# V of the later sequences by seven half-depth products, with its bias added by a transfer and its tokens turned by VectorE

## The chip, the cores and the metric

The kernel runs on one core of one Trainium2 chip. A core has five engines with instruction queues of their own: TensorE (PE; its weight loads are shown apart as PEld), VectorE (DVE), ScalarE (ACT), GpSimd (POOL) and SyncE (SP), which here only issues transfers. Sixteen DMA engines move data between the chip's memory (HBM) and the on-chip buffers. Matmul results go to PSUM, of which this kernel uses eight banks of 128 x 512 float32 in turn. The metric is the device time in microseconds, the median of several executions. The profile comes from one further execution; its span reaches from the first to the last instruction.

## The reference

Four sequences of 2048 tokens with 512 columns pass through one transformer block: layer norm, attention with 16 heads of 32 columns, and beside it two experts out of eight, chosen by the first token of each sequence. All is float32.

```python
xn = layernorm(x)                                  # x: 4 x 2048 x 512
q, k, v = split(xn @ qkv_w.T + qkv_b)              # 16 heads of 32
att = softmax(q @ k.T / sqrt(32)) @ v
o1 = att @ proj_w.T + proj_b
e = top_2(xn[:, 0] @ Wr + br)                      # two experts for each sequence
o2 = mean over e of (gelu(xn @ W1[e] + b1[e]) @ W2[e] + b2[e])
out = x + o1 + o2
```

## The kernel before

**Units.** The attention is cut into 1024 units. A unit is one group of four heads, one chunk of 512 queries and one tile of 128 keys; 16 units make a chunk, 64 units a group (four chunks), 256 units a sequence (four groups). One loop over `U` (L898) writes out every engine's instructions in order (the schedule is by hand), from 22 lead-in steps below zero to 1023. In a unit TensorE lays the negative maxima into four PSUM banks by a bf16 product (`shift`, L773), adds the scores (`score`, L781), and computes the plain scores of a unit 22 steps later (`score_max`, L763), whose maxima VectorE takes (L925). ScalarE makes the exponentials `p` (L918). In even units TensorE weighs V with the two latest `p` tiles (`weigh`, L793). POOL adds up the `p` tiles of a chunk (`add_weights`, L804 to L820); the last tile of a chunk is added by an accumulating transfer instead (L818). `add_keys` (L822) then sums over the keys on TensorE, four or five units into the next chunk. There are four `p` buffers.

**Dense items.** Odd units (and lead-in steps) are slots for one dense item each, after the attention's own work: projections `qk` and `v`, the experts' `w1` and `w2`, and the output projection `proj`. `Plan` (L38) fixes the slots of `qk` and `v`, and fills the rest from two queues of parts in order of their due times; some slots stay empty, spread evenly over slots at the sixth unit of a chunk (`rests`). Every item issues its matmuls in fours side by side (`product`, L499): four weight loads of 32 columns each, each with a moving operand of 512 columns. An fp32 matmul of the program is two matmul instructions in the profile.

**Seven products.** `qk` and `w1` are already computed with seven instead of eight half-depth products of 2 x 2 blocks. The combined blocks of tokens (`tx`, `token_blocks`) and weights (`ws`, `weight_blocks`) are made by POOL and stored to HBM; a product loads its two blocks (`load_xt`, `load_wt`) and `combine` (L535) adds the result into the outputs. `GAPS` (L31) lists which products share a slot. V is not done so: `project_v` (L526) takes all 512 rows of depth in one product for 128 tokens, adds the bias on VectorE (L532) and stores 256 KB to `v_dram`, from where each group loads its 128 columns (`v`, four buffers).

**The next sequence's tokens.** While a sequence is in its second and third group, the next one is normalised: statistics (`stats`), one square root for all (`root`, L450), `normal` on ScalarE, and `turn` (L469): four transposes of 128 x 128 on TensorE into a bank, a copy by VectorE (L474) into a staging tile, and at a chunk's end a store of 1 MB to `xn_dram`. ScalarE must load another function table for the square root and for Gelu, and again for the exponential (`back_to_exp`, L690).

**Planned loads.** Each load is issued by SyncE, in order, up to eight units ahead of its use or when its buffer comes free (`loads`, L225). What is to be stored goes through `later`, one to four units behind its work. The rows that collect the output get their biases in HBM by an accumulating transfer on POOL's queue (`add_bias`, L697).

Of the kernel before, what the change touches and what calls it, by code (L numbers as in the profile page):

```python
# [30 lines left out]
GAPS = [[(1, 0)], [(1, 1)]] + [[(i, 0), (i, 1)] for i in (6, 7)]  # L31
GAPS += [[(5, h), (3, h)] for h in (0, 1)] + [[(i, 0), (i, 1)] for i in (4, 2)]
COMBINED = (0, 1, 1, 2)
STORED = 6
# [3 lines left out]
class Plan:  # L38
# [5 lines left out]

    def __init__(self, B, DC, NCH, NT, TPC):
        self.per_group = NCH * NT
# [12 lines left out]
        for G in range(1, B * DC):  # L59
            b, g = divmod(G, DC)  # L60
            first = (G - 1) * self.per_group
            for n, products in enumerate(GAPS):
                at = (11, 12, 13, 14, 15, 16, 17, 19) if g else (5, 6, 7, 8, 9, 11, 12, 13)
                fixed[first + 2 * at[n] + 1] = ("qk", b, g, products)
            if g == 0:
                at = [n for n in range(14, 32) if n % 8 != 2]
                for t in range(NT):
                    fixed[first + 2 * at[t] + 1] = ("v", b, t)
        v_stored = {}
        for s, item in fixed.items():  # L70
            if item[0] == "v":
                v_stored[item[1], item[2] // TPC] = s + 3
        for b in range(B):
            for g in range(DC):
                for c in range(NCH):
                    self.first_load["v", (b, g, c)] = v_stored[b, c]
        for b in range(1, B):
# [8 lines left out]
            for n in range(NT):  # L86
                self.extra.setdefault(q1 + 2 * (16 + n) + 1, []).append(("stats", b, n))
                c, i = divmod(n, TPC)
                at = q2 + 2 * (1 + 18 * (c // 2) + 5 * (c % 2) + i) + 1
                self.extra.setdefault(at, []).append(("normal", b, n))  # L90
                self.extra.setdefault(at + 2, []).append(("turn", b, n))
            self.extra.setdefault(q2 + 1, []).append(("root", b, 0))
            for p in range(NCH // 2):
# [8 lines left out]
        for p, at in enumerate((slots[8], slots[16])):  # L102
            for n in range(4):
                self.extra.setdefault(at + n, []).append(("tx", 0, (p, n)))
            for i in STEPS:
                self.first_load["xt", (0, p, i)] = at + 5
        for k, at in enumerate((slots[2], slots[7])):
            for n in range(4):
                self.extra.setdefault(at + n // 2, []).append(("ws", 0, (k, n)))
            for i in STEPS:  # L110
                self.first_load["wt", ("w1", 0, k, i)] = at + 4
# [26 lines left out]
        free = [s for s in slots if s > 0 and s not in fixed]  # L138
        rests = [s for s in free if s % NT == 5]
        share = spare / len(rests)  # L140
        current, before, owed = [], None, 0
        for s in slots:
# [7 lines left out]
            )  # L150
            before = None
            if s in rests:
                owed += share
# [12 lines left out]
        for s in range(NT, self.units, NT):  # L166
            ends = s + NT == self.units
            self.keys_at[s // NT - 1] = 5 if s + 5 not in self.items and not ends else 4
        assert not fixed and not proj and not ffn and not current, (proj, ffn, current)

        rows_at = {}
        for s in slots:
            for it in self.items.get(s, []):
                if it[0] == "w2":
                    rows_at[it[1], it[3]] = s + 3
                assert it[0] != "proj" or s - 2 * WARN >= rows_at[it[1], it[2]], (s, it)
                for tag, key in self.needs(it):
# [7 lines left out]
        for s in range(slots[0], self.units):  # L185
            for kind, b, n in self.extra.get(s, []):
                if kind == "ws":

                    last = n[1] == 3
                    self.uses.append((s + (2 if b == 0 else 4) * last, "xl", ("w1raw", b, n[0])))  # L190
                elif kind == "tx" and b:
                    for c in (2 * n[0], 2 * n[0] + 1):
                        self.uses.append((s + 4 * (n[1] == 3), "xq", ("stage", b, c)))
                elif kind in ("stats", "normal"):
                    self.uses.append((s, "xl", (kind, b, n // TPC)))
                elif kind == "turn":
                    self.uses.append((s, "xq", ("stage", b, n // TPC)))
        self.uses.append((self.units, "wb", ("proj",)))
# [9 lines left out]
    def needs(item):  # L208
# [5 lines left out]
        if kind == "v":  # L214
            return [("wb", ("v",))] + ([("xq", (b, item[2] // TPC))] if b else [])
        if kind == "w1":
# [8 lines left out]
    def loads(self, bufs, start):  # L225
# [3 lines left out]
        for s, tag, key in self.uses:  # L229
# [9 lines left out]
            for t in tiles:  # L239
                if t[0] == key:  # L240
                    t[1] = s + 2 if tag in ("row", "prow") or tag == "xq" and key[0] == "stage" else s
        return {at: sorted(v, key=lambda e: e[0]) for at, v in out.items()}


@with_exitstack
def block_kernel(
# [45 lines left out]
    for b in range(B):  # L292
# [3 lines left out]
        tc.dram_tile([3, GH * TPC, TPC, HD], BF16, name=f"parts_dram_{n}") for n in range(2)  # L296
    ]
    wqk_dram = [tc.dram_tile([P, DC, D], F32, name=f"wqk_dram_{n}") for n in range(2)]
    for b in range(B):
        for c in range(NCH):  # L300
            xn_dram[b, c] = tc.dram_tile([P, DC, CH], F32, name=f"xn_dram_{b}_{c}")
            v_dram[b, c] = tc.dram_tile([P, TPC, D], F32, name=f"v_dram_{b}_{c}")
# [7 lines left out]
    BUFS = {"xq": 2, "xt": 4, "xl": 1, "wt": 4, "v": 4, "wb": 2, "row": 4, "prow": 2}  # L310
    held = {}
    experts = {}
# [9 lines left out]


    def load_xt(t, b, p, i):

        if i in (1, 2, 3):
            src, h = xn_dram[b, 2 * p + (i == 3)], int(i != 1)
        else:
# [3 lines left out]
    def load_wt(t, kind, b, n, i):  # L332


        r, h = {1: (0, 0), 2: (0, 1), 4: (1, 1), 6: (0, 0), 3: (0, 1), 7: (1, 0), 5: (1, 1)}[i]
        if kind == "qk":
            if i in (1, 2, 4):
# [15 lines left out]
    def load(tag, key):  # L353
# [4 lines left out]
        held[tag, key] = t  # L358
        if tag == "xq" and key[0] == "stage":
            return t  # L360
        if tag == "xq":
            nc.sync.dma_start(t, xn_dram[key])
        elif tag == "xt":
# [105 lines left out]
    def turn(dst, t, i, name):  # L469
# [4 lines left out]
        nc.vector.tensor_copy(dst[:, :, ts(i, P)], pt.rearrange("p (d t) -> p d t", d=DC))  # L474


    mv, sd, nb = stat_tiles("first")
# [57 lines left out]
    def combine(i, x, c, b1, b2, on_dve):  # L535

        add = nc.vector.tensor_tensor
        biased = nc.vector.scalar_tensor_tensor
        if i == 1 and on_dve:
# [7 lines left out]
        elif i == 5:  # L547
            biased(c[1, 1], x, b2, c[1, 0], ALU.add, ALU.add)
            add(c[0, 1], x, c[0, 1], ALU.add)
        else:  # L550
            at, b_ = {3: ((0, 1), b1), 4: ((1, 0), b2), 2: ((0, 0), b1)}[i]
            biased(c[at], x, b_, c[at], ALU.add, ALU.add)

# [25 lines left out]

    stage = {}  # L580

    def blocks(kind, b, n, U):


        if kind == "tx":
            p, n = n
# [20 lines left out]
    def dense(item, U, on_dve, between):  # L607
# [20 lines left out]
        elif kind == "v":  # L628
            n = item[2]
            project_v(b, n, tiles[1] if b else stage[0, n // TPC], tiles[0], U)  # L630
        elif kind == "w1":
# [83 lines left out]
    def first_turn(c):  # L715
# [5 lines left out]
        for i in range(TPC):  # L721
            turn(xn, x_first[c][:, i, :], i, f"0_{c}_{i}")
        nc.sync.dma_start(xn_dram[0, c], xn)

# [79 lines left out]
    def add_weights(u):  # L804
# [9 lines left out]
        elif kt == 1:  # L814
            psums[b, g, qc] = pair.tile([P, GH, CH], F32, tag="psum", name=f"psum_{b}_{g}_{qc}")
            nc.gpsimd.tensor_tensor(psums[b, g, qc], pT[u - 1], pT[u], ALU.add)  # L816
        elif kt == NT - 1:
            nc.gpsimd.dma_start(psums[b, g, qc], pT[u], accum_op=ALU.add)  # L818
# [69 lines left out]

    row_ready = {}
    loads = plan.loads(BUFS, -LEAD - 1)  # L890
# [7 lines left out]
    for U in range(-LEAD, plan.units):  # L898
# [43 lines left out]

        two = any(it[0] in ("qk", "w1") and len(it[-1]) == 2 for it in plan.items.get(U, []))
        if not two:
# [5 lines left out]
        if second:  # L950
            add_weights(U)
        for t in row_ready.pop(U, []):
            nc.gpsimd.tensor_tensor(t, t, bias[0], ALU.add)
# [5 lines left out]
        for u in (U - 2, U - 3):  # L959
            late = u + 3 < plan.units and u + 3 not in plan.items  # L960
            if u % 2 == 0 and u >= plan.units - NT and late == (u == U - 3):
                add_last(u)
        if before is not None and kt == keys:
            add_keys(before, bank("keys_%d_%d_%d" % before), [psums[before]], False)
        for step, sb, n in plan.extra.get(U, []):
            if step == "stats":
                if n == 0:
                    norms[sb] = stat_tiles(sb)
                stats(norms[sb][0], n, held["xl", ("stats", sb, n // TPC)][:, n % TPC, :])
            elif step in ("ws", "tx"):  # L970
                blocks(step, sb, n, U)
# [5 lines left out]
            else:  # L977
                c, i = divmod(n, TPC)
                xs = stage[sb, c] = held["xq", ("stage", sb, c)]
                turn(xs, held["xl", ("normal", sb, c)][:, i, :], i, f"{sb}_{n}")  # L980
                if i == TPC - 1:
                    later(U + 1, lambda sb=sb, c=c, xs=xs: nc.sync.dma_start(xn_dram[sb, c], xs))
        for item in plan.items.get(U, []):
            dense(item, U, curve is not None, invert if two else lambda: None)

# [111 lines left out]
```

## Time and profile before

| | us |
|---|---|
| median of three runs | 4973.19 (4972.93 to 4974.06) |
| the profiled execution | 4967.9 |
| its span | 4966.1 |
| mean granted TensorE clock, share of full | 0.999 |
| vector additions of psum on POOL, L820 | 3724.0 busy, 819 of 4.547 |
| accumulating transfers psum<-p, landing | 63, median 8.6 |
| DMA queue of SP, share of 16 engines' span | 31.7% |

The profile's busy time of a group is the union of its instructions' times, so side-by-side matmuls count once. In a row of a group the number behind the bar is busy time in microseconds and the mean of one instruction in ns; then the idle time of the engine ahead of the group, and what ended it. "vps" are V's results in PSUM, "xt" both the banks of turned tokens (L473) and the loaded token blocks, "xq" 1 MB buffers of tokens.

### The profile page before, as it was taken

To read this page: it belongs to the slowest core of one execution; us is meant where nothing else is said; L and a number is where in the kernel's file an instruction comes from. 1 tells how busy PE (TensorE), PEld (TensorE's weight loads), DVE (VectorE), ACT (ScalarE), POOL (GpSimd) and SP (SyncE) were. 2 spreads that over 40 slices of the span, in tenths; PEclk is the share of its full clock that TensorE was granted. 3 is DMA by queue.
4 is the path that set the end of the run, shared out by engine and by line. 5 is a ranking of instruction groups with operands and counts; after the bars stand their busy time and mean duration, and the time that the engine had idled before them with its cause. 6 is when DMAs were issued, how large, how long until landed. Compare 5 with 4: busy or idle time off the path is not lost.

```text
span 4966.1 us, 108027 instructions
## 1 busy us (share of the span) xinstructions
PE 4913.9 (99%) x44740; PEld 1712.0 (34%) x44740; DVE 3714.2 (75%) x5899; ACT 2491.9 (50%) x4570; POOL 4403.5 (89%) x1469
## 2 busy tenths in 40 slices
PE   8999999999999999999999999999999999999999
PEld 2333333333333333333333333333333333333332
DVE  5777787777777787777777778877777777777772
ACT  1445456464444545454455445555544445555553
POOL 2799999999898998999988998999988988989983
PEclk9999999999999999999999999999999999999999
DMA  6334337433333434634234244564423343323323
GB/s 225 113 106 120 112 99 196 150 121 110 82 107 104 131 109 139 187 122 137 88 94 132 73 128 128 171 167 131 145 70 98 106 129 107 95 81 112 87 81 101
DMA packets 327772, 594.93 MB, mean 120 GB/s; under 512 B 42220, under 2 KB 162540, under 8 KB 310384
## 3 DMA queue, kind: packets, MB, share of 16 engines
q1 hardware_dynamic: 311872, 509.37, 31.7%
q0 software_dynamic: 15408, 78.65, 8.2%
q8 instruction: 352, 5.77, 0.5%
q14 instruction: 140, 1.15, 0.1%
HBM read 380.81 MB, written 153.62 MB: 108 GB/s over the span
## 4 chain that ended last, share of the span: by engine, by line
PE 83%; ACT 6%; POOL 5%; issue 3%; DMA 2%; DVE 1%; SPq 0%; POOLq 0%; ACTq 0%
PE acc L793 17%; PE s L781 15%; PE m L763 15%; PE qkps L503 6%; PE ops L503 6%; PE hps L503 6%; PE s L773 6%; PE vps L503 5%; POOL psum L820 4%; PE prps L503 4%; ACT p L918 3%; DMA psum<-p 2%; PE keys L826 1%; ACT L692 1%; ACT h L922 1%
## 5 line engine op out<-in xcount | busy, mean ns | idle before, releaser
L820 POOL TENSOR_TENSOR psum<-psum,p 128x2048 f32<-128x2048 f32 x819 | 3724.0, 4547 | 158.3 <-ACT p L918 117.4
L918 ACT ACTIVATE p<-s 128x512 f32<-128x512 f32 x4096 | 2116.9, 602 | 2225.3 <-PE m L763 2062.8
L925 DVE TENSOR_REDUCE mx<-m 128x1 f32<-128x512 f32 x4096 | 2543.1, 683 | 569.2 <-PE m L763 567.4
L781 PE MATMUL s<-qT,kT 32*128 32x512 f32 x8192 | 1919.0, 588 | 0.0
L763 PE MATMUL m<-kT,qT 32*128 32x512 f32 x8192 | 1911.3, 590 | 3.9 <-DVE row L657 2.5
L763 PEld LDWEIGHTS m<-kT,qT 32*128 32x128 f32 x8192 | 921.8, 184 | 330.2 <-issue 240.5
L793 PE MATMUL acc<-p,v 128*32 128x512 f32 x8192 | 985.8, 599 | 9.6 <-ACT p L918 5.5
L781 PEld LDWEIGHTS s<-qT,kT 32*128 32x128 f32 x8192 | 768.1, 185 | 30.8 <-issue 9.2
L503 PE MATMUL ops<-wb_w,h 128*32 128x512 f32 x4096 | 466.0, 595 | 0.2 <-ACT p L918 0.2
L816 POOL TENSOR_TENSOR psum<-p,p 128x2048 f32<-128x2048 f32 x63 | 288.1, 4573 | 194.0 <-ACT p L918 194.0
L793 PEld LDWEIGHTS acc<-p,v 128*32 128x32 f32 x8192 | 214.0, 109 | 709.7 <-ACT p L918 392.8
L802 DVE TENSOR_TENSOR sacc<-acc,sacc 128x512 f32<-128x512 f32 x448 | 309.9, 692 | 139.9 <-PE acc L793 139.9
L773 PE MATMUL s<-negms,ones_b 32*128 32x512 bf16 x4096 | 406.2, 385 | 7.5 <-ACT p L918 7.0
L503 PE MATMUL hps<-xt,wt_w 128*32 128x512 f32 x3584 | 411.0, 596 | 1.1 <-ACT p L918 1.0
L773 PEld LDWEIGHTS <-ones_b 32*128 32x128 bf16 x4096 | 103.4, 91 | 858.0 <-issue 850.4
L503 PE MATMUL qkps<-xt,wt_qk 128*32 128x512 f32 x3360 | 386.7, 597 | 11.4 <-ACT p L918 11.4
L940 DVE RECIPROCAL sums<-sums 128x128 f32<-128x128 f32 x252 | 235.9, 936 | 0.7 <-ACT sums L838 0.7
L503 PEld LDWEIGHTS ops<-wb_w,h 128*32 128x32 f32 x4096 | 120.0, 109 | 314.7 <-issue 229.8
L657 DVE SCALAR_TENSOR_TENSOR row<-ops,row 128x512 f32<-128x512 f32 x128 | 88.5, 691 | 163.9 <-PE ops L503 153.6
L503 PE MATMUL prps<-wb_proj,xl_at 128*32 128x512 f32 x1792 | 203.9, 595 | 0.0
L503 PEld LDWEIGHTS hps<-xt,wt_w 128*32 128x32 f32 x3584 | 103.3, 109 | 276.2 <-issue 185.4
L503 PEld LDWEIGHTS qkps<-xt,wt_qk 128*32 128x32 f32 x3360 | 97.1, 110 | 283.6 <-issue 180.6
(127 smaller groups left out, 1975.6 us busy)
## 6 DMA issues: line engine op xcount, KB each, us to landing
xt<-t_dram SPq DMA_DIRECT2D x181, 512.0 KB
xt<-xn_dram SPq DMA_DIRECT2D x133, 512.0 KB
psum<-p POOLq DMA_DIRECT2D x63, 1024.0 KB, 8.6
part_dram<-row SPq DMA_DIRECT2D x128, 256.0 KB
v_dram<-v SPq DMA_DIRECT2D x64, 256.0 KB
wt_w<-ws_dram SPq DMA_DIRECT2D x128, 128.0 KB
v<-v_dram SPq DMA_DIRECT2D x64, 256.0 KB
row<-part_dram SPq DMA_DIRECT2D x64, 256.0 KB
```

Of the source, the lines that this page charges most:

```text
L503: nc.tensor.matmul(pp[rows_of(j), :], lhsT[:, rows_of(j)], rhs, start=(first and n == 0), stop=(last and n == len(terms) - 1),)
L657: nc.vector.scalar_tensor_tensor(row, pp, 0.5, row, ALU.mult, ALU.add)
L763: nc.tensor.matmul(t, qT[b, g, qc][r, ts(i, P)], kT[b, g, kc][r, :], start=True, stop=True)
L773: nc.tensor.matmul(tiles[j], ones_b[r, :], negm[b, g, qc][r, :], start=True, stop=False)
L781: nc.tensor.matmul(tiles[j], kT[b, g, kt // TPC][r, ts(kt % TPC, P)], qT[b, g, qc][r, :], start=False, stop=True,)
L793: nc.tensor.matmul(acc[r, :], held["v", (b, g, kt // TPC)][:, (kt + n) % TPC, r], pT[u + n][:, j, :], start=(n == 0), stop=(n == 1),)
L802: nc.vector.tensor_tensor(t, acc, t, ALU.add)
L816: nc.gpsimd.tensor_tensor(psums[b, g, qc], pT[u - 1], pT[u], ALU.add)
L820: nc.gpsimd.tensor_tensor(psums[b, g, qc], psums[b, g, qc], pT[u], ALU.add)
L918: nc.scalar.activation(pT[U][:, j, :], tiles[j], AF.Exp, scale=SCALE)
L925: nc.vector.tensor_reduce(dst, t, AX.X, ALU.max, negate=True)
L940: nc.vector.reciprocal(sums[before][:, q], sums[before][:, q])
```

## The change

V of sequences 1 to 3 is computed by seven half-depth products of 2 x 2 blocks: for each half of a sequence (1024 tokens), blocks of 512 tokens, 256 rows and 256 columns, each in two parts of 256 tokens. That makes 14 items of two products for each sequence in place of 16 items of one; they are the new kind `v7`, in slots fixed by `V_GAPS`. The moving operand of their matmuls has 256 columns. The results are collected in two 1 MB tiles of tag `xq`, stored to `v_dram` two units behind the last product, and two units later the bias is added there by POOL's accumulating transfer. V of sequence 0 stays as it was; its weights are then combined in place and stored.

The turn becomes a VectorE transpose of 32 x 32 blocks, whose four groups of 32 partitions are stored by four transfers in pieces of 32 floats; `xn_dram` gets another order for it, and the staging tiles are loaded from there. Further edits: slots of a chunk behind which blocks are combined no longer stay empty (`summed`); the root of a sequence, and its normalisations and turns, move by one slot where a Gelu falls on the root's slot (`late`; in this plan sequence 2 alone), and a dense item in the root's slot makes its copies on VectorE; and the last `p` tile of the chunk before the last is summed on TensorE rather than by the accumulating transfer.

```diff
+V_GAPS = [[(i, 0), (i, 1)] for i in (1, 6, 7)]
+V_GAPS += [[(5, h), (3, h)] for h in (0, 1)] + [[(i, 0), (i, 1)] for i in (4, 2)]
...
-                at = [n for n in range(14, 32) if n % 8 != 2]
-                for t in range(NT):
-                    fixed[first + 2 * at[t] + 1] = ("v", b, t)
+                for p, at in enumerate(((14, 15, 16, 17, 19, 20, 21), (24, 25, 27, 28, 29, 30, 31))):
+                    for n, products in enumerate(V_GAPS):
+                        fixed[first + 2 * at[n] + 1] = ("v7", b, p, products)
...
+            elif item[0] == "v7":
+                for c in (2 * item[2], 2 * item[2] + 1):
+                    v_stored[item[1], c] = max(v_stored.get((item[1], c), 0), s + 8)
...
-                at = q2 + 2 * (1 + 18 * (c // 2) + 5 * (c % 2) + i) + 1
+                at = q2 + 2 * (1 + (b in late) + 18 * (c // 2) + 5 * (c % 2) + i) + 1
...
-            self.extra.setdefault(q2 + 1, []).append(("root", b, 0))
+            self.extra.setdefault(q2 + 1 + 2 * (b in late), []).append(("root", b, 0))
...
-        rests = [s for s in free if s % NT == 5]
+        summed = {
+            (s + 1) // NT for s, steps in self.extra.items() for e in steps
+            if e[0] in ("ws", "tx") and s % NT == NT - 1
+        }
+        rests = [s for s in free if s % NT == 5 and s // NT not in summed]
...
+    def turn_blocks(b, n, U):
+
+        c, i = divmod(n, TPC)
+        t = pair.tile([P, D], F32, tag="vrow", name=f"turned_{b}_{n}")
+        nc.vector.transpose(t, held["xl", ("normal", b, c)][:, i, :])
+
+        def store():
+            dst = xn_dram[b, c].rearrange("d (e p) n -> p (d e) n", p=HD)
+            for a in range(P // HD):
+                nc.sync.dma_start(
+                    dst[:, :, i * P + a * HD : i * P + (a + 1) * HD],
+                    t[rows_of(a)].rearrange("p (de n) -> p de n", n=HD),
+                )
+
+        later(U + 1, store)
...
+        elif kind == "v7":
...
+                pp = bank(f"vps_{b}_{p}_{i}_{half}")
+                for t in range(2):
+                    rhs = pp[:, t * D // 2 : (t + 1) * D // 2]
+                    product(rhs, [
+                        (xt[:, d, ts(2 * half + t, P)], wt[:, d].rearrange("p q m -> p (q m)"))
+                        for d in range(2)
+                    ])
...
+                combine(i, x_, o, None, None, on_dve)
...
+            if products[-1] == (2, 1):
+                for c in range(2):
+                    later(U + 2, lambda c=c: nc.sync.dma_start(v_dram[b, 2 * p + c], values[c]))
+                    v_biases.setdefault(U + 4, []).append((b, 2 * p + c))
...
+        elif u == plan.units - NT - 1:
+            return
...
+        for n in v_biases.pop(U, []):
+            nc.gpsimd.dma_start(
+                v_dram[n], bv_bc.unsqueeze(1).to_broadcast([P, TPC, D]), accum_op=ALU.add
+            )
...
+        ends_soon = U >= plan.units - NT
+        if ends_soon and kt == 0:
+            add_keys(before, bank("keys_%d_%d_%d" % place(U)[:3]), [pT[U - 1]], False)
         if before is not None and kt == keys:
-            add_keys(before, bank("keys_%d_%d_%d" % before), [psums[before]], False)
+            add_keys(before, bank("keys_%d_%d_%d" % before), [psums[before]], ends_soon)
```

## The prediction

> **What bounds the kernel now.** First the page: busy time and the chain that ended last.
>
> ```profile
> span 4966.1 us, 108027 instructions
> ...
> PE 4913.9 (99%) x44740; PEld 1712.0 (34%) x44740; DVE 3714.2 (75%) x5899; ACT 2491.9 (50%) x4570; POOL 4403.5 (89%) x1469
> ...
> PE 83%; ACT 6%; POOL 5%; issue 3%; DMA 2%; DVE 1%; SPq 0%; POOLq 0%; ACTq 0%
> ```
>
> TensorE is idle for 52 us in all, so work taken from it shortens the run nearly one for one, until POOL (89%) or a single wait ends later. Then the groups that the change touches, from the page and the list by line:
>
> ```profile
> L503 PE MATMUL vps<-wb_v,xq 128*32 128x512 f32 x1536 | 174.7, 595 | 0.2 <-ACT p L918 0.2
> L473 PE MATMUL xt<-ident,xl_normal 128*128 128x128 f32 x192 | 31.5, 287 | 0.7 <-ACT p L918 0.7
> L474 DVE COPY xq_stage<-xt 128x512 f32<-128x512 f32 x56 | 36.6, 662 | 2.6 <-PE xt L473 2.6
> L532 DVE TENSOR_TENSOR v<-vps,bv_bc 128x512 f32<-128x512 f32 x64 | 44.3, 692 | 87.1 <-PE vps L503 84.1 <-DMA v_dram<-v 3.0
> L857 DVE STREAM_TRANSPOSE turned<-negs 128x32 f32<-128x32 f32 x64 | 13.6, 212 | 2.2
> L699 POOL DMA_DIRECT2D base_dram<-bias x12 | 15.5, 2358 | 0.0
> L488 PE MATMUL route_ps<-wr_sb,firstT 128*4 128x8 f32 x8 | 0.4, 172 | 0.3 <-DVE firstT L485 0.3
> ```
>
> Busy time hides how long a step holds TensorE. The pieces of the chain show it for V, TensorE's timeline for a turn:
>
> ```profile
> 1185.53 3.57 PE vps L503 x32
> 1189.10 0.33 PE s L773 x4
> ...
> 1195.04 3.57 PE vps L503 x32
> ```
>
> ```profile
> 768.55 0.66 PE L473 MATMUL xt<-ident,xl_normal 128*128 128x128 f32 x4
> 769.14 0.64 PE L503 MATMUL hps<-xt,wt_w 128*32 128x512 f32 x4
> ```
>
> The second fence is of one engine's timeline. A V item takes 3.57 us, with other TensorE work directly behind it; a turn delays the next item by 769.14 - 768.55 = 0.59 us. Last, where TensorE does stand: ScalarE's timeline at the two longest waits behind the start-up.
>
> ```profile
> 2342.68 1.57 ACT L918 ACTIVATE p<-s 128x512 f32<-128x512 f32 x3 [7.98 <-DMA psum<-p]
> ```
>
> ```profile
> 4880.86 1.57 ACT L918 ACTIVATE p<-s 128x512 f32<-128x512 f32 x3 [8.39 <-DMA psum<-p]
> ```
>
> Both times the exponentials want one of the four p buffers that the accumulating transfer at a chunk's end still reads; TensorE stands 6.0 us in each.
>
> **The change, part by part.**
>
> *V.* 48 items (three later sequences, 16 each) become 3 x 14 = 42. Each new item is two products of 256 tokens x 256 columns at half depth: 32 matmul instructions of 256 columns each where an old item had 32 of 512, side by side in fours, so two products hold 3.57 us if half the columns take half the time. TensorE loses (48 - 42) x 3.57 = 21.4 us. That condition is the main unknown. Below: nothing is gained beyond half[...]. Above: in the V stretch (1185.53 to 1261.50 in the windows) 708 matmuls and 712 weight loads went by in 75.97 us, 53.5 ns an instruction, and no long stretch is denser; if that were a limit, a product's 64 instructions would take 3.42 us instead of 1.79. The nearest rows: the eight route_ps matmuls, each with a weight load of its own, span 0.35 us in the timeline, less one's 0.17 is 0.18/7 = 25 ns a pair; a product needs a pair per 1.79/32 = 56 ns. The Trainium skill (TensorE: Matmul & The Clock Gate, Back-to-back issue gap) speaks against the change: it gives about 81 ns for each weight load with its matmul at 128 columns in a sustained stream. By that a product would take 32 x 81 = 2.59 us, and V 84 x 0.80 = 67 us more than my sum. I take the row, because four loads here fill four strips side by side, and keep the rule for a rival.
>
> VectorE gets 84 combining steps for 48 additions of 0.692 us: about 59 against 33 us, and ScalarE 12 copies of some 0.6 us. Both lie beside TensorE: in that V stretch VectorE was busy for 54.8 of 76.0 us. Cover gone, it is 26 us.
>
> *Turns.* 48 x 0.59 = 28.3 us leave TensorE. VectorE has 48 transposes of 128x512 for 48 copies of 0.66. Bounds: 0.21 us (the 32-column row) to twice a full-width row, 1.4; I take 0.7, as that row plus 480 more columns at the pace of a 512-column operation. That is 2 us more, hidden. A late one would hold the maxima behind it on VectorE, and through their PSUM banks TensorE.
>
> *Stores of turned tiles.* Four transfers a tile, 2048 pieces of 128 bytes. No such store is in the trace. Nearest row, the DMA view of 1922.9 to 1924.7 us, which holds one load in 512-byte pieces:
>
> ```profile
> DMA packets 528, 0.26 MB, mean 146 GB/s; under 512 B 16, under 2 KB 528, under 8 KB 528
> ...
> q1 hardware_dynamic: 528, 0.26, 49.6%
> ```
>
> 0.496 x 1.8 us x 16 / 528 = 27 ns a packet; a tile takes 2048 x 27 / 16 = 3.5 us of all engines. By bytes alone it is 0.9. The Trainium skill (DMA: Bandwidth & Descriptors, Specifications) says that pieces below 512 bytes are read, changed and written back. At twice the row that is 7 us. What each makes of it is read from the windows:
>
> ```profile
> 742.40:824.20 81.80, 79.53 (x704) 28.04 (x700) 61.73 (x98) 49.29 (x85) 79.10 (x31) 1.00 0.64 199
> 824.20:896.80 72.60, 72.19 (x668) 26.04 (x668) 57.15 (x90) 43.55 (x77) 66.27 (x24) 1.00 0.70 168
> ```
>
> The last columns are clock, DMA share and GB/s. Four tiles fall into each: by the row the second share rises by 14/72.6 to 0.89, by the rule to 1.09, a backlog of 6.5 us that loads would meet, and the shift rows (stored four, fetched three units before use). I take the row. In SyncE's queue, 192 stores at about 0.4 us stand before later loads; most loads go eight units (39 us) ahead.
>
> *The bias of V.* Twelve accumulating transfers on POOL's queue, 15.5/12 = 1.3 us each, two together, six times: 2.6 us ahead of the next psum addition, inside POOL's slack. The first also waits for the V store, with the psum additions, and so the p buffers, queued behind it; the store goes two units earlier. Landing: 13.8 to 35.1 us in the four-in-a-row of base_dram (view of that tensor). For the second half of V it is issued three units into the sequence and V is read at the tenth, 7 x 4.85 (4966/1024) = 34 us later; 4.6 for the addition ahead, 22 for the second of a pair and about 3 for the load leave 4 us. SyncE stands meanwhile for some 2 units, and loads behind it have that much. I cost it at nothing; at 35 us it is 9 x 3 = 27.
>
> *Weights of V* are combined once, four POOL steps of 2.4 us in the lead-in, where POOL is some 20% busy (page, first slice): nothing. Some 32 MB of extra loads: nothing by itself.
>
> *Single waits.* The wait at 2343 us: the chunk ahead ran 66.9 us against about 75.6 of POOL work, because two slots lay empty; in the new plan it holds one item more (3.6 us). Saved 3.6, and 1.7 more since the clock in 2331 to 2416 was 0.98 (0.02 x 85). At 4881 the transfer is replaced by 8 matmuls, 1.0 us: net -4. Moving the square root of one sequence away from a Gelu: TensorE stood 2.1 us there; saved 1. Sum -10.3. For new short waits (negms behind the stores; one xt load of the second half two units ahead; POOL's 2.6 us) I add 5.
>
> **Sum.** -21.4 - 28.3 - 10.3 + 5 = -55 us: 4967.9 to 4913 for the profiled execution. That lies 5.3 us under the median of 4973.2, so 4918 there. Within 0.2% (10 us) this kernel can't be told from no change.
>
> **Rivals.** A, the other side: TensorE is held by its instruction rate in the short products. For it: nothing in the trace sustains more than one per 53.5 ns, and the rule. Against it: 25 ns a pair, and eight weight loads of 0.11 us each that are over in 0.16 (weight loads' timeline at 769.13). Time: at 81 ns a pair 4918 + 67 = 4985, at 53.5 ns an instruction 4918 + 84 x 1.63 = 5055. It decides from 56 + 55,000/(84 x 32) = 76 ns a pair. Chance 0.12.
> B: small stores saturate the DMA engines; 6.5 us and one more late load of about 2 per sequence, 3 x 8.5: 4943. For it the 0.64 and 0.70 above; against it, the waits on negms so far are below 2 us in all. Chance 0.13.
> C: POOL becomes the bound in the chunks where token and weight blocks are combined (three places; POOL 14 x 4.55 + 3.3 + some 8 of blocks, 75 us, against TensorE's 71 to 74): up to 6 us each, as at 2343, so 4936. Against it, from 1050 to 1124 us the two were level, and nothing stood. Chance 0.08.
> D: V or its bias comes late, and gains and losses cancel: 4970. Chance 0.05.
> The likeliest, 4918, keeps 0.62; its own range is 4903 to 4936. 4900 to 4955 takes in B and C and leaves A and D out. Faster 0.80 (likeliest, B, C, less tails), same 0.06, slower 0.14.
>
> **What would show it.** vps of later sequences: 2688 matmuls of 256 columns, an item of two in 3.5 to 3.6 us; over 5 says A. The xt group of later sequences is gone, the span of TensorE's busy time near 4860. The DMA share below 1 in the turning chunks, and no new TensorE wait on negms or v above 2 us, says not B. ACT waiting for psum over 10 us in a chunk says C. A forecast of this kind is wrong if TensorE's idle time grows by over 40 us.

## The result, and the profile after

The changed kernel takes 4982.91 us (median of 17 runs, 4979.28 to 4987.80), the kernel before 4973.19 in 17 runs beside it (4970.38 to 4978.18). The ratio is 1.0018, with a 95% interval of 1.0012 to 1.0025: a small loss (the quickest run after, 4979.28, lies above the slowest before, 4978.18), where a gain of 55 us was forecast. The profiled execution has a span of 4978.1 us, 12.0 more than before, and its clock is 0.995.

First the page of the changed kernel, busy time and the chain that ended last:

```profile
span 4978.1 us, 110401 instructions
...
PE 4894.6 (98%) x45708; PEld 1739.5 (35%) x45708; DVE 3739.3 (75%) x5941; ACT 2494.5 (50%) x4577; POOL 4422.8 (89%) x1484
...
PE 80%; ACT 6%; POOL 5%; DMA 4%; issue 2%; DVE 2%; SPq 1%; POOLq 0%; ACTq 0%; DVEq 0%
```

TensorE is busy for 19.3 us less and yet idle for 83.5 us (4978.1 - 4894.6) where it was 52.2. Next the list of groups by line and shape, for the two things that the change was to make cheap:

```profile
L561 PE MATMUL vps<-wt_v,xt 128*32 128x256 f32 x2688 | 153.7, 381 | 0.2 <-ACT p L1014 0.2
L522 DVE STREAM_TRANSPOSE turned<-xl_normal 128x512 f32<-128x512 f32 x48 | 33.0, 688 | 27.7 <-DMA xn_dram<-turned 27.7
```

And a piece of the chain in the V stretch:

```profile
1193.06 3.59 PE vps L561 x64
```

The 84 short products go at the hoped pace: an item of two takes 3.59 us, 56 ns for each weight load with its matmul. The transpose takes 0.69 us on average, also as expected. But the second row's last part is new: VectorE stood 27.7 us ahead of these transposes, waiting for transfers out of the tile `turned`. The waits of the changed kernel (total us, times, longest):

```profile
DVE turned L522 <- DMA xn_dram<-turned: 27.7, 4, 9.7
PEld L867 <- DMA negms<-parts_dram: 7.9, 7, 5.2
PE prps L561 <- DMA wb_proj<-in_proj_wT_dram: 3.4, 1, 3.4
```

Four waits, three of them of about 9 us. The timelines of one, in order SyncE, VectorE, TensorE (start, duration, instruction, and in brackets the idle time ahead and what ended it):

```profile
826.07 13.83 SPq L527 DMA_DIRECT2D xn_dram<-turned  x4
839.97 4.54 SPq L381 DMA_DIRECT2D wt_qk<-wqk_dram  x1
```

```profile
855.89 0.71 DVE L522 STREAM_TRANSPOSE turned<-xl_normal 128x512 f32<-128x512 f32 x1 [8.86 <-DMA xn_dram<-turned]
856.53 0.65 DVE L751 SCALAR_TENSOR_TENSOR row<-ops,row 128x512 f32<-128x512 f32 x1
857.11 1.87 DVE L1021 TENSOR_REDUCE mx<-m 128x1 f32<-128x512 f32 x3
```

```profile
857.24 2.07 PE L857 MATMUL m<-kT,qT 32*128 32x512 f32 x2 [7.19 <-DVE row L751]
```

The four stores of one turned tile hold SyncE for 13.83 us. The tile's buffer (one of two) is still being read at 847, when VectorE reaches the turn two tiles later; the chain of this stretch has the store that ends last in flight until 855.77 us:

```profile
831.49 24.28 DMA xn_dram<-turned
```

VectorE works in order, so an addition (`row`) and the maxima stand behind the turn; their PSUM banks stay full, and TensorE stands 7.19 us. The same happens at 2077 us (6.37) and at 3284 us (7.31). The granted clock makes each of them longer, as the windows of the stretch behind this one show (columns: busy us and instructions of PE, PEld, DVE, ACT, POOL; then the clock, the DMA share, GB/s):

```profile
853.50:863.70 10.20, 6.46 (x26) 1.76 (x30) 4.46 (x7) 0.00 (x0) 2.70 (x1) 0.50 0.76 197
863.70:880.00 16.30, 16.30 (x156) 5.73 (x152) 13.45 (x22) 9.46 (x18) 13.07 (x3) 1.00 0.62 211
```

For 10 us the clock was halved, and 6.46 us of TensorE's work in them would have taken about half.

**Why just there.** POOL's timeline of the changed kernel shows what was in flight:

```profile
821.61 0.90 POOL L914 DMA_DIRECT2D psum<-p  x1 [0.30 <-POOL psum L916]
822.25 5.17 POOL L793 DMA_DIRECT2D base_dram<-bias  x4
```

Four accumulating transfers of 1 MB each, the biases of the next sequence's rows, are issued 4 us ahead of the tile's stores. They are issued at 2039.7 us and from 3247.1 us too, ahead of the other two. By issue and landing time the last of each four lands at 855.55, 2074.23 and 3281.78 us, and VectorE's three turns start at 855.89, 2075.74 and 3282.22: the wait ends when these transfers do. The kernel before has them as well; its DMA view of 826 to 856 us (the share of each queue in 16 engines) could have been read before the change:

```profile
q0 software_dynamic: 2065, 4.69, 88.7%
q1 hardware_dynamic: 1052, 1.81, 18.7%
```

For 30 us the accumulating transfers take nearly all sixteen engines. Among the waits of the kernel before there is none of VectorE on such a store.

**Where the 12.0 us come from.** The span is TensorE's busy time plus its idle time, and the busy time holds what the halved clock cost: by estimate half of the busy time in the windows with clock 0.5 (before the last stores). In us of profiled executions:

| kernel | work at full clock | lost to clock | idle | span |
|---|---|---|---|---|
| before | 4910.4 | 3.5 | 52.2 | 4966.1 |
| repairs alone (e4) | 4911.7 | 6.8 | 46.3 | 4964.8 |
| repairs and V (e1) | 4897.2 | 3.4 | 52.0 | 4952.6 |
| after: repairs, V, turns | 4874.0 | 20.6 | 83.5 | 4978.1 |
| after, four buffers (e3) | 4872.2 | 11.9 | 68.3 | 4952.4 |
| the same and two remedies (e9) | 4877.3 | 4.5 | 53.8 | 4935.6 |

From before to after, 36.4 us of work are gone; 31.3 of idle time and 17.1 of clock have come.

### The profile page after: what moved, and what is told of

It reads as the page before. It is cut to its first block, busy times and chain, and to the rows that moved or that the text cites. A ratio compares the mean times of both kernels' runs of the same rounds, so it can differ in the third digit from the quotient of the medians.

```text
span 4978.1 us, 110401 instructions
## 1 busy us (share of the span) xinstructions
PE 4894.6 (98%) x45708; PEld 1739.5 (35%) x45708; DVE 3739.3 (75%) x5941; ACT 2494.5 (50%) x4577; POOL 4422.8 (89%) x1484
## 4 chain that ended last, share of the span: by engine, by line
PE 80%; ACT 6%; POOL 5%; DMA 4%; issue 2%; DVE 2%; SPq 1%; POOLq 0%; ACTq 0%; DVEq 0%
PE acc L887 17%; PE s L875 15%; PE m L857 14%; PE qkps L561 7%; PE ops L561 6%; PE s L867 6%; PE hps L561 5%; POOL psum L916 5%; PE vps L561 4%; PE prps L561 4%; ACT p L1014 3%; DMA psum<-p 2%; PE keys L922 1%; ACT L786 1%; DVE mx L1021 1%
## 5 line engine op out<-in xcount | busy, mean ns | idle before, releaser
L887 PE MATMUL acc<-p,v 128*32 128x512 f32 x8192 | 989.4, 600 | 13.8 <-ACT p L1014 9.6
```

Of the source, the lines that this page charges most:

```text
L887: nc.tensor.matmul(acc[r, :], held["v", (b, g, kt // TPC)][:, (kt + n) % TPC, r], pT[u + n][:, j, :], start=(n == 0), stop=(n == 1),)
```

## The experiments

All ratios are to the kernel before in the same job, with 95% intervals. Where an edit is called "after, but", it starts from the changed kernel.

### The parts by themselves

**e1: after, but turns by TensorE.** V and the repairs stay.

```diff
-                turn_blocks(sb, n, U)
+                c, i = divmod(n, TPC)
+                xs = stage[sb, c] = held["xq", ("stage", sb, c)]
+                turn(xs, held["xl", ("normal", sb, c)][:, i, :], i, f"{sb}_{n}")
```

> The changed kernel with its turns given back to TensorE (four transposes and a VectorE copy, one 1 MB store for each chunk), V's seven products and the repairs kept. Theory S (the 128-byte pieces of the turned tiles' stores fill the DMA engines, VectorE's next turn waits for its buffer, TensorE behind it): the turning stretches come back to their old length less what the repairs give, so about 4950 us (V -21, repairs -10, new short waits +8 against 4973). Theory V (the V products with their loads and bias transfers cost as much as they save): 4965 or more.

4954.39 us, 0.9964 (0.9951 to 0.9978). So the part that turned the gain into a loss is the turn by VectorE, with its stores.

**e4: before, with the repairs alone** (`summed`, `late`, copies on VectorE in the root's slot, the last chunk's keys).

```diff
-        rests = [s for s in free if s % NT == 5]
+        rests = [s for s in free if s % NT == 5 and s // NT not in summed]
...
+        elif u == plan.units - NT - 1:
+            return
```

> The kernel before with the repairs alone: no empty slots in chunks behind which blocks are combined, root and turns of sequence 2 a slot later, copies on VectorE in the root's slot, the last chunk's transfer replaced by TensorE. By the prediction's sum 4963 us (-10.3). If the repairs only move the waits: 4970 to 4976.

4964.04 us, 0.9985 (0.9978 to 0.9991): 8 us in the medians. The profiled executions show less of it, 1.3 us: idle time is down by 5.9, lost clock up by 3.3 and work by 1.3 (table). One repair did not do what it was for: with sequence 2's root moved by a slot (`late`), a Gelu still stands directly ahead of the root in ScalarE's timeline, and TensorE's stand there is 2.07 us where it was 2.08. V by itself is then e1 against e4, some 10 us in the medians.

### What makes the turn dear

**e2: after, but turned tiles stored in rows of 2 KB.** The order of the tokens in `xn_dram` isn't the one that is read, so later sequences are computed from rearranged values; the transfers and everything else keep their number and size.

```diff
-                nc.sync.dma_start(
-                    dst[:, :, i * P + a * HD : i * P + (a + 1) * HD],
-                    t[rows_of(a)].rearrange("p (de n) -> p de n", n=HD),
-                )
+                nc.sync.dma_start(dst[i * P + a * HD : i * P + (a + 1) * HD, :], t[rows_of(a)])
```

> The changed kernel, but each turned tile is stored by the same four transfers in whole rows of 2 KB instead of pieces of 128 bytes, so the next sequence's tokens stand in the wrong order in HBM and the output is not the reference's; bytes, number of transfers, queues and every other instruction stay. Theory S: the loss in the turning stretches goes, 4935 us (4925 to 4945), VectorE's turn no longer waits for xn_dram<-turned. Theory T (the turn on VectorE costs by its place in VectorE's queue and by the staging loads, whatever the pieces): 4975 or more.

4951.31 us, 0.9965 (0.9951 to 0.9978). With two buffers still, VectorE waits 1.7 us in all for them; the stores hold SyncE for at most 3.2 us each. The time stays 6 us above the range that was expected.

**e3: after, but four buffers for turned tiles**, the pieces left at 128 bytes.

```diff
-        t = pair.tile([P, D], F32, tag="vrow", name=f"turned_{b}_{n}")
+        t = pair.tile([P, D], F32, tag=("vrow", "turnrow")[n % 2], name=f"turned_{b}_{n}")
```

> The changed kernel, 128-byte pieces kept, with four buffers for turned tiles instead of two (the tags vrow and turnrow by turns). If only the wait of VectorE's turn for its buffer costs, the time is that of whole rows, 4950 to 4957. If the pieces cost by the transfers' own rate too (SyncE's queue and later loads stand behind them), between 4962 and 4980.

4954.55 us, 0.9967 (0.9954 to 0.9980). The list of this kernel's turn:

```profile
L527 SPq DMA_DIRECT2D xn_dram<-turned x192: 302/504/8827, 772.1 to 3423.0; - x192
L522 DVE STREAM_TRANSPOSE turned<-xl_normal x48: 650/700/711, 771.4 to 3418.6; 128x512 f32<-128x512 f32 x48
```

(least, median and longest duration in ns.) A store still holds SyncE for up to 8.8 us, but VectorE waits for no buffer any more, and the time is that of the 2 KB rows. What cost 28 us by the medians of two jobs (4982.9 against 4954.6), or 25 by the ratios (1.0018 against 0.9967), was thus VectorE waiting in its queue for a buffer. The small pieces cost through that wait: with rows of 2 KB two buffers were enough (e2), with four buffers the pieces did no such harm.

**e5: after, but four turned tiles collected, stored in pieces of 512 bytes.** The tokens are permuted when they are loaded, so that four tiles give whole pieces; a chunk is stored by four transfers in place of 16.

```diff
-            nc.sync.dma_start(t, x_rows(*key[1:]))
+            for a in range(GH):
+                nc.sync.dma_start(t[rows_of(a)], x_turned(*key[1:])[a])
```

> The changed kernel with the tokens of a chunk loaded in another order (partition 32a+n of tile i holds token 128a+32i+n), so that the four turned tiles of a chunk lie together in a 1 MB buffer and are stored in pieces of 512 bytes, four transfers a chunk instead of sixteen. Theory S: 2048 pieces a chunk at 27 ns are 3.5 us of all engines, so the loss goes as with whole rows: 4935 us (4925 to 4945). Theory T: 4975 or more.

4957.17 us, 0.9972 (0.9960 to 0.9983). No VectorE wait for a buffer, and no better than e3; this too is above what was expected.

**e13: after, but the bias transfers eight units later**, between two stretches of turns. Two buffers and 128-byte pieces as in the change.

```diff
-        if g == 2 and qc == 1 and kt == 0 and second and b + 1 < B:
+        if g == 2 and qc == 1 and kt == 8 and second and b + 1 < B:
```

> The changed kernel, with two buffers for turned tiles and 128-byte pieces as it is, but the four accumulating transfers that add the biases to the next sequence's rows (base_dram<-bias) issued eight units later, between the two stretches of turns rather than in the middle of one. Theory (they fill the DMA engines for some 30 us, the turned tiles' stores wait behind them, VectorE waits for the buffers): VectorE's waits for turned buffers fall from 27.7 us to below 5, TensorE's stands at units 150, 407 and 663 (7.2, 6.4 and 7.3 us) and the halved clock behind them go, and the time is about that of the four-buffer kernel, 4950 to 4957. Rival (128-byte pieces are slow by themselves): VectorE still waits 15 us or more, and the time stays above 4970.

4971.78 us, 0.9997 (0.9988 to 1.0006). The waits of this kernel:

```profile
DVE turned L522 <- DMA xn_dram<-turned: 0.3, 1, 0.3
PEld L867 <- DMA negms<-parts_dram: 18.1, 12, 5.2
```

VectorE's wait fell from 27.7 to 0.3 us, and the stands at units 150, 407 and 663 are gone: the collision was with these transfers. The time did not follow as forecast: idle time (74.9 us) and lost clock (15.2) fell only part of the way. At units 415 and 671 TensorE now stands 2.87 and 2.73 us for the row of maxima, whose fetch meets the moved transfers (the last of them lands at 2109.2 and 3310.2 us). At unit 163 it stands 3.20 us for an accumulating `p` transfer; that one is issued at 902.8 us, behind the landing of the last bias transfer (896.4), so it does not meet them in flight. Their issue took 4.85 us of POOL's queue in this chunk; whether that is what made the `p` transfer late was not tried.

### Where the turns' 25 us of TensorE work went

With its buffers repaired, the turn by VectorE takes 25.0 us of work off TensorE (4897.2 - 4872.2) and yet e3 and e1 have the same time. The rows that got worse are the stands behind the chunk-end transfers: ScalarE's waits for `psum<-p` are 37.5 us in e1 and 49.6 in e3, and TensorE's stand at 399 for the row of maxima 1.7 and 4.3 us.

**e6: e5, and the last `p` tile of chunks 7, 9, 12, 15, 16, 26, 41, 44 and 62 summed by TensorE** in place of the accumulating transfer.

```diff
-        elif u == plan.units - NT - 1:
+        elif kt == NT - 1 and u // NT in KEYED:
             return
...
-        ends_soon = U >= plan.units - NT
+        ends_soon = chunk - 1 in KEYED
```

> The kernel with long pieces (512 bytes), and at the ends of eight more chunks (7, 9, 12, 15, 16, 26, 41, 44, where the exponential waited 1.6 us or more for the chunk's accumulating transfer) the last p tile is summed on TensorE, as the change does for the chunk before the last. Theory P (with less TensorE work these transfers end last, and TensorE's clock is halved for some microseconds behind each stand): 8 x 0.93 us more TensorE work, 18 us of stands and some 5 us of halved clock less, so 4941 against 4957. If the stands only move to the next wait: 4955 to 4960.

4949.65 us, 0.9956 (0.9942 to 0.9969). Of ScalarE's 54.5 us of waits for `psum<-p` in e5, 10.6 are left, and a new stand of 7.25 us came at unit 407 for a token block's load. That load was issued at 2041.1 us, behind the collected store, and landed at 2062.7, 0.3 us after the last of the four bias transfers, which points to the same collision with a load as its victim.

**e7: e6, and the output projection's weights issued ahead of a unit's stores.**

```diff
+        for s, tag, key in loads.get(U, []):
+            if tag == "wb":
+                load(tag, key)
         for do in waiting.pop(U, []):
             do()
```

> As the kernel with keyed ends, and the loads of 1 MB weight blocks are issued ahead of a unit's stores, so that the output projection's weights of sequence 3 (used two units later) do not stand behind the 2 MB of V's store. Theory: TensorE's 2.9 us stand at unit 771 and the halved clock behind it go: 4936, 5 below keyed ends. If the load waits for its buffer and not for the store: no difference.

4946.60 us, 0.9942 (0.9928 to 0.9956). No stand for `wb_proj` is left at 771, but e6 has none there either (1.28 us, for ScalarE); those at 399 and 407 stay. The runs of e7 (4934.85 to 4950.00) and e6 (4944.46 to 4952.86) overlap, so a gain of this edit by itself is not shown.

**e8: e5, and the token blocks of later sequences combined by VectorE**, to see whether POOL's load is behind the late `p` transfers.

```diff
-        sub = nc.gpsimd.tensor_tensor
+        sub = nc.vector.tensor_tensor if b else nc.gpsimd.tensor_tensor
```

> The kernel with long pieces, with the token blocks of later sequences combined on VectorE instead of POOL (24 operations of 128x1024). Theory C (POOL is behind TensorE in the chunks where blocks are combined, so that the chunk's transfer starts late): the stands of units 163, 211, 435, 675 and 723 shrink, 4949 against 4957. If the transfer's own landing is the wait, or VectorE's queue pays it back: 4955 to 4962.

4987.56 us, 1.0039 (1.0026 to 1.0053). The group of plain scores in this kernel:

```profile
L865 PE MATMUL m<-kT,qT 32*128 32x512 f32 x8192 | 1935.7, 592 | 20.4 <-DVE kT L621 9.8 <-DVE row L759 5.8 <-DVE h L609 4.9
```

ScalarE's waits for `psum<-p` fell from 54.5 us (e5) to 26.0, but TensorE now stands behind VectorE. Fewer of the late transfers, paid for elsewhere: VectorE's 25% of idle time is no room for blocks of 1.2 to 3.6 us in front of the maxima. How much of the fall is due to POOL's smaller load stays open, since a run that is 30 us longer gives POOL more time as well.

**e9: e3 with both remedies** (chunks 7, 12, 15, 22, 26, 44, 62). The edits are those of e6 and e7.

> The changed kernel with four buffers for turned tiles, the last p tile of chunks 7, 12, 15, 22, 26, 44 and 62 summed over the keys by TensorE itself instead of by an accumulating transfer, and output-projection weights issued ahead of a unit's stores. Theory (what V and the turns take off TensorE is handed back as stands at chunk ends, plus the halved clock behind stands of 2 us or more): the four-buffer kernel's stands at units 131, 211, 259, 371, 435 and 723 (13.5 us in its trace, and some 6 us of clock) go, against six extra sums of 1.0 us each, so 4941 to 4946; clock loss below 5 us; the stand at unit 399 for the row of maxima (4.3 us) stays. Rival (the stands only move, because POOL or the transfers behind it set the pace over whole stretches): 4951 to 4956, with new stands of the same sum elsewhere.

4937.4 us (4934.85 to 4941.28), 0.9934 (0.9920 to 0.9947): the quickest measured. ScalarE's waits for `psum<-p` are 20.9 us, the lost clock 4.5, and the work is 5.1 us up for the extra sums.

**e11: e1 with both remedies** (chunks 7, 15, 16, 22, 51, 62), to see what the turn is worth where its side costs are gone.

> The changed kernel with turns on TensorE again (as e1_turns_tensor), with the same two remedies: the last p tile of chunks 7, 15, 16, 22, 51 and 62 summed on TensorE, output-projection weights ahead of the stores. This asks what the turn on VectorE is worth once the stands at chunk ends are gone in both. Theory (24.5 us of TensorE work really left with the turns and can be cashed once nothing stands): 4947 to 4951, that is some 5 us or more above e9_four_keyed. Rival (the turn on VectorE is worth nothing in any case, because its stores and the VectorE queue hand the time back): equal to e9_four_keyed within 2 us.

4947.32 us, 0.9954 (0.9940 to 0.9968). So the turn by VectorE is worth 10 us in e9, of the 25 it takes off TensorE; TensorE's idle time is still 12.1 us longer than in e11 (53.8 against 41.7). In the change as it was made it cost 28 (4982.9 against e1's 4954.4, two jobs).

### Trials on the last stands

**e10: e9, but sequence 2's root and turns not shifted by a slot.**

```diff
-        if again and not late:
+        if again and not late and False:
```

> The kernel of the run e9_four_keyed with the root, normalisations and turns of sequence 2 left in their old slots (no shift by one slot). If the shift is what makes the row of maxima late at unit 399 (4.3 us there and some 4 us of halved clock), that stand falls below 1 us and the time is 4 to 8 us below e9_four_keyed, less some 2 us if the root meets the Gelu again. If the shift is harmless, the time is within 2 us of e9_four_keyed, or up to 3 us above it, and the stand at 399 remains.

4938.54 us, 0.9940 (0.9927 to 0.9954). The stand at 399 stayed (6.35 us): the shift is not its cause.

**e12: e9, with the row of maxima ahead in its unit.** In e9, SyncE issued its fetch behind a turned tile:

```profile
2006.21 3.68 SPq L966 DMA_DIRECT2D parts_dram<-parts  x4
2010.20 4.65 SPq L528 DMA_DIRECT2D xn_dram<-turned  x4
2015.52 1.52 SPq L973 DMA_DIRECT2D negms<-parts_dram  x4
```

```diff
-            later(U + 3, pending[1])
-            later(U + 4, pending[2])
+            waiting.setdefault(U + 3, []).insert(0, pending[1])
+            first[U + 4] = pending[2]
```

> The kernel of the run e9_four_keyed with only the order of SyncE's queue within a unit changed: the stores and fetches of a chunk's row of maxima stand ahead of what else the unit issues. In e9_four_keyed's trace the fetch at unit 399 was issued 4.9 us late, behind one turned tile's four stores, which held SyncE for 4.65 us. Theory (the stores of 128-byte pieces hold SyncE's queue, and the row of maxima behind them): the stand of 4.4 us there falls below 1.5 us and its 3.4 us of clock go, so 4930 to 4935. Rival (the row is late because its own transfers are slow among the small ones): the stand stays above 3 us and the time within 2 us of e9_four_keyed, 4937.

4940.3 us, 0.9934 (0.9921 to 0.9948). A miss: the turned tile's stores belong to the unit ahead of the fetch, so the fetch still stood behind them (3.30 us), and TensorE stood 4.31. Both readings of that stand stay open.

**e14: e9, with the bias transfers eight units later.** The edit is that of e13.

> The kernel of the run e9_four_keyed with the same four transfers eight units later. Theory: there the row of maxima at unit 399 (4.4 us, and 3.4 us of clock) is late for the same collision only if these transfers are in flight when it is fetched; they are issued 3.5 us behind that fetch, so the stand may stay. Expected 4934 to 4938, or 4929 to 4933 if the stand goes. Rival (with four buffers the collision costs nothing more, and the moved transfers press on the second stretch of turns): 4938 to 4945.

4952.95 us, 0.9965 (0.9951 to 0.9978), about 15 us worse than e9. With four buffers the old place does no harm to VectorE, while the new one costs three stands of 3 us (units 163, 415, 671) and their clock. Of the two places tried, the old one is the better with four buffers.

## Why the prediction was wrong

**The step that failed** is the one on the stores of turned tiles. It saw that the DMA share might rise from 0.70 to 0.89 by the row, or to 1.09 at twice the row, and took the row; and of a late turn it said that it "would hold the maxima behind it on VectorE, and through their PSUM banks TensorE", and put no price on it. Two things were wrong in it. A mean share over a chunk of 73 us was asked of a queue that fills in 30. The size was even too high: by the packet records of the trace a piece of 128 bytes took 13.8 ns where the row had 27, so a tile takes 1.8 us of all engines and not 3.5, and the share over the chunk of the first stand (816.8 to 903.5 us) was 0.79. But the accumulating bias transfers stood in the same trace, with landing times of 13.8 to 35.1 us that the prediction used for V's bias alone. And late transfers were thought to hurt loads; the first thing that they held was a buffer, two deep, of an instruction in VectorE's own queue. Its price: three stands of 6.4 to 7.3 us, other waits and the halved clock behind them, 25 to 28 us by e3.

**The rest, point by point.**

- *V, 21.4 us.* The items' pace is right (3.59 us for 3.57), and V's own matmuls fell by 21.0 us (174.7 to 153.7). TensorE's work fell by 14.5 (e1 less e4); of the difference of 6.5, some 4.6 lie in the scores (`m` and `s`), as many as before but longer by that, if each instant at full clock is given to the matmul that began first; why, the runs do not show. Idle time grew by 5.7, among it 2.65 at unit 771 for `wb_proj`, behind V's stores. In the medians some 10 us were left. The condition that the prediction called the main unknown held, and rival A with it fell: 81 ns a pair, which the Trainium skill (TensorE: Matmul & The Clock Gate, Back-to-back issue gap) gives for 128 columns, would by estimate have made an item of 64 pairs 5.2 us long.
- *Turns, 28.3 us.* The size was right: by the same count the transposes held 28.3 us in e1. The work fell by 25.0, as the plain scores took 3.4 more. Their value was the failed step, and then the stands at chunk ends.
- *Repairs, 10.3 us.* 8 us in the medians (e4), 1.3 in the profiled executions; ScalarE's long wait at 4881 us is gone in the changed kernel. The 1 us for moving the root did not come: the stand of 2.1 us is in every one of the sixteen traces, with the root moved or not (e10).
- *New short waits, 5 us.* Right in kind (`negms`, `wb_proj`, `psum<-p`), too small in size: in e3, which has no buffer wait, idle time and lost clock exceed e1's by 24.8 us, as much as the turns saved.
- *V's bias, POOL, the weights, VectorE's combining steps.* Costed at nothing. No TensorE wait on the loads of V appears; e8 speaks for a part of POOL's blocks in the late `psum<-p`, so the nothing for POOL was probably too little.
- *Rivals.* B (small stores and DMA engines) named the right neighbourhood, but with saturation by the small stores, a price of 25 us and another victim, a late load (such a one came at unit 407 in e6 and e7); C's waits came (`psum<-p` 33.9 to 41.7 us), smaller than its 6 us a place. The side of the result was given to A, whose mechanism did not happen.
- *What would show it.* "Idle time grows by over 40 us" was the sign of a wrong forecast; it grew by 31.3, and with the clock by 48.4. The sign left the clock out.

The forecast's sum of -55 against +12.0 in the spans is then: 36.4 of work gone, where the forecast had 21.4 and 28.3, and 31.3 of idle time and 17.1 of clock added, where it had 10.3 of old waits saved and 5 of new ones.

## What to carry to other kernels

When a step moves from TensorE to an engine that works in order, ask how many buffers its output has and what else is on the DMA queues while they drain; a mean DMA share over a chunk does not answer that, the view of the 30 us around it does. Work taken off the engine that sets the pace is only worth what the next wait leaves: here 25 us were worth nothing until the chunk-end transfers were taken away too, and then 10.

## What the runs showed of the hardware

- *Short stands can halve the clock, depending on where they fall.* The Trainium skill (TensorE: Matmul & The Clock Gate, HAM oscillation — how this bites in real kernels) warns of idle gaps above about 3.4 us. Here 2.07 us can be enough. TensorE's timeline and the windows of e1:

```profile
1967.05 1.12 PE L855 MATMUL m<-kT,qT 32*128 32x512 f32 x2 [2.07 <-DVE row L749]
```

```profile
1965.49:1968.90 3.41, 1.81 (x10) 0.58 (x14) 2.71 (x6) 3.37 (x7) 1.10 (x3) 1.00 0.20 77
1968.90:1972.31 3.41, 3.41 (x20) 0.88 (x16) 1.18 (x2) 0.72 (x2) 2.61 (x1) 0.51 0.58 132
1972.31:1975.72 3.41, 3.41 (x36) 1.29 (x32) 2.48 (x4) 2.73 (x6) 2.43 (x2) 0.99 0.99 333
```

In the middle window TensorE is busy all the time and finishes 20 matmuls where the next one has 36. In the kernel before, the same stand left the clock at 1.00:

```profile
1957.66 1.12 PE L763 MATMUL m<-kT,qT 32*128 32x512 f32 x2 [2.08 <-DVE row L657]
```

This stand (2.06 to 2.08 us) is in all sixteen traces; half clock followed in ten and not in six, nor behind one of 3.38 us in the changed kernel (unit 771), while one of 1.70 us in e4 (2032.7 us) was followed by 3.41 us of it. Much of what tells them apart is in the clock records: apart from the start and the last stores, the half-clock stretches last 3.41, 6.83 or 10.24 us, and within one execution they all begin on one grid of 3.41 us. Worked out from the sixteen traces, a step of this grid at full clock in which TensorE was busy for under 40% was followed by half clock every time (50 of 50), one with 40 to 65% in 15 of 94 cases, one with 65 to 85% never (251). A stand of 2.07 us takes 61% of a step if it falls into one, and less of each if it falls on a border. By the page's gap of 3.4 us only four stands of the changed kernel would have cost clock, by estimate 11.0 of its 20.6 us.

- *A store of small pieces can hold the issuing queue.* One of the 192 stores of 64 KB in pieces of 128 bytes took SyncE from 0.30 to 8.8 us to issue in e3, with a median of 0.50; four in a row took 13.83 and 18.03 us in the changed kernel (at 826 and 2053 us) while accumulating transfers filled the engines. In e2, with rows of 2 KB, the longest was 3.2; in e13, with the small pieces but these transfers moved, 2.8.
